# Two half blocks of y share their PSUM banks, and the image of both comes behind the products of both

## The chip, the cores and the metric

The kernel runs on one core of one Trainium2 chip. Its time is the device time of one execution in microseconds (us); the time before is the median of three runs. A profile is one further execution, taken by the hardware profiler, with start and duration of every instruction. The engines are TensorE (PE, with its weight loads shown apart as PEld), VectorE (DVE), ScalarE (ACT), GpSimd (POOL) and SyncE (SP, which only issues transfers here).

## The reference

The input x has 256 channels ("tokens") of 256 by 256 points, stored as (1, 256, 256, 128). Layer 0 is a gated attention with a residual sum; its result x1 goes to DRAM. Layer 1 is a Fourier neural operator on 256 tokens of 256 by 128 points. Cut to what matters here:

```
def spectral_conv(x, wr, wi, bias, out_hw):
    xf = rfft2(x); keep the low modes; mix them by w = wr + 1j * wi
    return irfft2(of) + bias
def fno_layer(x, ...):
    skip = einsum('bihw,oi->bohw', x, sw) + sb
    xf = spectral_conv(...); y = instance_norm(xf) + skip     # then gelu in the first of two
```

An attention over tokens comes first. In the kernel its skip part and the residual are folded into one matrix over tokens, mpT, and its spectral part into a small set of modes. Their sum is **y**, the quantity that the change is about: y = (mpT applied to x1) + (image of the modes), scaled per channel, together with the mean and variance of y for the norm that follows.

## The kernel before, in words

Everything is float32. Tokens stand on the 128 partitions, in two halves a = 0 and 1. A half of y has 32 half blocks u of 8 rows by 128 points (1024 columns, name HB), two of which are a block b of 16 rows (NB = 2048 columns).

`y_blocks` (line 1308) is a generator that makes one half block per step:

- **load**: two transfers on SP bring the half block of x1 for both token halves (tile xt, three buffers); for every even u four transfers bring the block's modes (tile gs, three buffers). They are asked for two half blocks ahead.
- **products** (line 1332): for each of four row classes j, two matmuls with 128 by 128 weights over 256 columns, summed in bank j. A float32 matmul shows as two records, so a half block has 16.
- **image** (line 1336, its matmul at line 1200): eight matmuls with 32 rows of weights, of which the four of different j run in different quarters of the array and write to four banks. Again 16 records.
- **eviction** (line 1342): DVE multiplies each bank's 256 columns by a row vector and writes to the kept array `blocks` (half 0) or to a tile yt (half 1, two buffers).
- **statistics** (line 1344): two bn_stats on DVE.
- **store** (line 1346, half 1 only): POOL issues a transfer of yt to the DRAM array yd.

The order of the work on each engine is the order in the program (`manual_schedule`). Half 0 runs alone, in a pool of eight banks, so two half blocks are in flight. Half 1 has one set of four banks ("r"), since the other four ("q") hold the modes' work. `weave(main, side)` (line 1231) mixes its half blocks into another generator: `main` yields the time that it expects PE to be free, `side` the time of its step, and steps of `side` are placed while time is due. The first 24 half blocks are woven into `first_modes(0)`: a chain of statistics, the mixing of modes (`mix_modes`, line 1349: 16 products named x0m, every third on POOL and the others on DVE, each summed by a matmul with the identity at line 1381, tile x0acc), the squares (x0sq) and norm (x0ens), and four chunks of synthesis (`synth_modes`, tile g10gp, line 576) with a small reduction at lines 1471 to 1489 behind the second chunk. What is left of the 24 runs alone. Then `first_images(0)` follows (line 1491: tile ups, ACT's gelu, a sum w of x1 and y with loads xw that use the buffers of yt). The last eight half blocks are woven into the start of `second_modes(0)` (line 1585: f1ps, z0m, z0acc).

Each step waits only by tile: a matmul that starts in a bank waits until that bank's last reader is done, an eviction into yt until the store of that buffer has landed.

Of the kernel before, what the change touches and what calls it, by code (L numbers as in the profile page):

```python
# [10 lines left out]
FP = mybir.dt.float32  # L11
AF = mybir.ActivationFunctionType
ALU = mybir.AluOpType
# [5 lines left out]
P = 128  # L19
# [3 lines left out]
def bc(ap, axis, n):  # L23

    a = ap.unsqueeze(axis)
    shape = list(a.shape)
    shape[axis] = n
    return a.to_broadcast(shape)
# [484 lines left out]
def layer1(tc, I, C, ident, x1d, upool, U, stats2, mv2, out):  # L513
# [6 lines left out]
    nc = tc.nc  # L520
    NT, H, W = 256, 256, 128
    L = lambda n: I["L1_conv_" + n]
    with ExitStack() as ctx:
# [10 lines left out]
        rwb = keep.tile([P, W], FP, name="rwb")  # L534
        bsy = keep.tile([P, W], FP, name="bsy")
# [112 lines left out]
        with tc.manual_schedule(engines=COMPUTE):  # L648
# [306 lines left out]
            ps = psa.tile([P, 512], FP, tag="a", name="gtps")  # L955
# [12 lines left out]
            mpT = late.tile([P, 2, NT], FP, name="mpT")  # L968

            for t in range(2):  # L970
                for b in range(2):
                    ps = psa.tile([P, 512], FP, tag="a", name=f"fvps_{t}_{b}")
# [19 lines left out]
        xp = yctx.enter_context(tc.tile_pool(name="xp", bufs=2))  # L992

        def load_x1(a, u):

            t = xp.tile([P, 2, NB // 2], FP, tag="xt", name=f"xt_{a}_{u}", bufs=3)
            for sc in range(2):
                nc.sync.dma_start(t[:, sc], x1v[:, sc, u * NB // 2 : (u + 1) * NB // 2])
            return t
# [109 lines left out]
        with tc.manual_schedule(engines=COMPUTE):  # L1109
# [33 lines left out]
            ps = psa.tile([P, 512], FP, tag="a", name="mbps")  # L1143
# [20 lines left out]
            for c in range(4):  # L1164
                ps = psa.tile([P, 512], FP, tag="a", name=f"fyps_{c}")
# [15 lines left out]
        ydv = yd.rearrange("(a p) x -> p a x", p=P)  # L1181
        outv = out.rearrange("(a p) h w -> p a (h w)", p=P)
        HB = NB // 2
        big = ctx.enter_context(tc.tile_pool(name="big", bufs=1, side="right"))
        blocks = big.tile([P, 16, NB], FP, name="blocks")
        hb = [blocks[:, b, :] for b in range(16)]

        def by_turn(t):

            return t.rearrange("p (n j w) -> p j n w", j=4, w=W)  # L1190

        def rows_of(ps):
            return ps.rearrange("p (n w) -> p n w", w=W)

        def image(ps, gs, bs, rows=range(4)):

            for k, n in enumerate(rows):
                for j in range(4):
                    q = slice(32 * j, 32 * j + 32)
                    nc.tensor.matmul(  # L1200
                        ps[j][:, k * W : (k + 1) * W], gs[q, n, :], bs[q, :],
                        start=False, stop=(k == len(rows) - 1),
                    )
# [16 lines left out]
        def load_modes(gs, Gd, b, tt=None):  # L1220
            for j in range(4):
                q = slice(32 * j, 32 * j + 32)
                if tt is None:
                    nc.sync.dma_start(
                        gs[q].rearrange("f n t -> f (n t)"),
                        Gd[:, j, 4 * b : 4 * b + 4, :].rearrange("f n t -> f (n t)"),
                    )
                else:
                    nc.sync.dma_start(gs[q], Gd[:, j, 4 * b : 4 * b + 4, tt])
# [19 lines left out]
        ystat = sp.tile([P, 2, 64, 6], FP, name="ystat")  # L1249
        with tc.tile_pool(name="psb", bufs=4, space=PSUM) as psa:  # L1250

            ps = psa.tile([P, 512], FP, tag="a", name="chps")
# [4 lines left out]
            ps = psa.tile([P, 512], FP, tag="a", name="blkps")  # L1257
# [50 lines left out]
        def y_blocks(a, psum, lo, hi, kept=16):  # L1308

            tt = slice(a * P, (a + 1) * P)  # L1310
            gs = {}

            def load(u):
                if (a, u) not in xts:
                    xts[a, u] = load_x1(a, u)
                if u % 2 == 0:
                    gs[u // 2] = xp.tile([P, 4, P], FP, tag="gs", name=f"gs_{a}_{u}", bufs=3)
                    load_modes(gs[u // 2], Gd0, u // 2, tt)

            load(lo)  # L1320
            load(lo + 1)
            yield 0.0
            for u in range(lo, hi):
                b, s = u // 2, u % 2
                if u + 2 < hi:
                    load(u + 2)
                xt = xts.pop((a, u))
                ps = [psum.pool.tile([P, 512], FP, tag=psum.tag, name=f"yps_{a}_{u}_{j}") for j in range(4)]
                ps = [z[:, 0:256] for z in ps]
                for j in range(4):  # L1330
                    for sc in range(2):
                        nc.tensor.matmul(  # L1332
                            rows_of(ps[j]), mpT[:, sc, tt], by_turn(xt[:, sc])[:, j],
                            start=(sc == 0), stop=False,
                        )
                image(ps, gs[b], bsy, range(2 * s, 2 * s + 2))
                if a == 0:
                    yt = blocks[:, b, s * HB : (s + 1) * HB]
                else:
                    yt = xp.tile([P, HB], FP, tag="yt", name=f"yt_{u}")  # L1340
                for j in range(4):
                    nc.vector.tensor_tensor(by_turn(yt)[:, j], rows_of(ps[j]), bc(rwb, 1, 2), ALU.mult)  # L1342
                for g in range(2):
                    nc.vector.bn_stats(ystat[:, a, 2 * u + g, :], yt[:, g * 512 : (g + 1) * 512])
                if a:
                    nc.gpsimd.dma_start(ydv[:, a, u * HB : (u + 1) * HB], yt)  # L1346
                yield 4.2

        def mix_modes(mk, acc, F, l, tag, cs):

# [445 lines left out]
        with tc.manual_schedule(engines=COMPUTE | {ENG.SP}):  # L1796
            with tc.tile_pool(name="psy", bufs=8, space=PSUM) as psy:
                run(y_blocks(0, Banks(psy, "y"), 0, 32))
# [6 lines left out]
            with yctx:  # L1805
                U1 = 24
                with tc.tile_pool(name="mp0", bufs=1) as wp:
                    y1 = y_blocks(1, br, 0, U1)
                    weave((2.4 * t for t in first_modes(0, wp, tiles(wp), bq, [(wp, "gt", 1)])), y1)
                    run(y1)  # L1810
                with tc.tile_pool(name="hp0", bufs=2) as wp:
                    run(first_images(0, wp, xp, bq, br))
                with tc.tile_pool(name="mp1", bufs=1) as wp:
                    y1 = y_blocks(1, br, U1, 32)
                    next(y1)
                    m0 = second_modes(
                        0, wp, tiles(wp), bq, [(xp, "xt", 3)], [(wp, "gt", 1)] * 3 + [(xp, "xt", 3)]
                    )
                    weave((2.4 * next(m0) for _ in range(3)), y1)
                    run(y1)  # L1820
                    m1 = first_modes(
                        1, wp, Tiles(F=(xp, "yt", 2), f=(xp, "yt", 2), m=(xp, "gs", 3)), br, [(xp, "xt", 3)]
                    )
                    next(m1)
                    for k, _ in enumerate(iter(lambda: next(m0), None)):
                        if k % 4 == 3:
                            next(m1)
                    for _ in m0:
                        next(m1, None)
                    o0 = output_0(bq)  # L1830
                    next(o0)
                    y2 = wp.tile([P, NB], FP, tag="gt", name="y2_0", bufs=1)
                    nc.sync.dma_start(y2, ydv[:, 1, 0:NB])
                    run(m1)
                    g2 = wp.tile([P, 4, P], FP, tag="m", name="gs2_1_0", bufs=2)
                    next(o0)
                    load_modes(g2, halves[1].Gd1, 0)
                    next(o0)
# [14 lines left out]
            with tc.tile_pool(name="op1", bufs=2, side="right") as op:  # L1853
                o1 = Output1(op)
                with tc.tile_pool(name="mp3", bufs=1) as wp, tc.tile_pool(
                    name="mpq3", bufs=8, space=PSUM
# [14 lines left out]
                with tc.tile_pool(name="opk1", bufs=8, space=PSUM) as psk, tc.tile_pool(  # L1871
                    name="op2", bufs=1
# [165 lines left out]
```

## Time and profile before

| what | value |
|---|---|
| median of three runs | 2890.68 us (2889.41 to 2895.76) |
| the profiled execution: its time | 2890.7 us |
| its span, first to last instruction | 2888.9 us |
| PE / DVE / ACT / POOL busy in the span | 2651 / 2008 / 1491 / 1680 us |
| half 0 of y | 1900.2 to about 2040 us |
| half 1, first 24 half blocks, woven and alone | 2039.6 to 2200.1 us |
| half 1, last eight half blocks | 2335.7 to 2390.6 us |
| line 1332, products of y | 1024 records, 247.7 us busy |

Times in the profile are us from the span's start, unless they are marked ns. A row of the timeline gives start, length, engine, line, operation, tiles, shape, and in square brackets how long the engine was idle before it and what ended that. A merged row of matmuls ends with the last one's drain, so its length exceeds the distance to the next row's start; distances between starts are used below. The granted clock is the share of TensorE's full clock. The chain that ended last spreads over very many short pieces (its largest entry is 5% of the span, PE), so the stretches have to be read one by one.

### The profile page before, as it was taken

Reading aid. Unit: us, or ns where it says so; the run is one execution under the profiler, and the core shown is the slowest. Engines: PE = TensorE matmul, PEld = TensorE weight load, DVE = VectorE, ACT = ScalarE, POOL = GpSimd, SP = SyncE. Lnnn points to the kernel's source line nnn. Section 1 sums busy time; section 2 is a strip of 40 time slices with the busy share of each in tenths; the row PEclk is TensorE's granted clock in tenths of the full one; section 3 lists DMA queues with packets and bytes.
Section 4 is the critical chain, followed back from the end, with each engine's and each line's share of the span. In section 5 each row is a group of like instructions: output and inputs, shape, how many; then the busy total and the mean of one; then the engine's idle time right before and its main releaser. Section 6 shows DMA issues by size and latency. Waiting matters only on the chain. (4 is left out here: it accounts for less than half of the span.)

```text
span 2888.9 us, 71477 instructions
## 1 busy us (share of the span) xinstructions
PE 2651.2 (92%) x29116; PEld 1941.7 (67%) x29116; DVE 2008.1 (70%) x3263; ACT 1491.0 (52%) x2849; POOL 1679.9 (58%) x1308
## 2 busy tenths in 40 slices
PE   6799999999999999999999899999889988799654
PEld 6677777777777777777777656778665555455532
DVE  7788888888888888888888744756645545365555
ACT  0477777777777777777777622200004611365132
POOL 0399999999999999999999800200114833111211
PEclk9999999999999999999999989999989989799865
DMA  9422222222222222222222101188879984798599
GB/s 369 164 67 67 67 67 67 67 67 67 67 68 69 68 67 69 68 66 71 67 67 67 41 19 53 34 278 271 277 236 319 310 296 137 251 360 305 187 359 337
DMA packets 246705, 430.12 MB, mean 149 GB/s; under 512 B 26278, under 2 KB 174201, under 8 KB 239976
## 3 DMA queue, kind: packets, MB, share of 16 engines
q1 hardware_dynamic: 206568, 335.34, 34.8%
q0 software_dynamic: 22912, 81.80, 7.4%
q10 hardware_dynamic: 16896, 8.39, 1.0%
q8 instruction: 231, 3.78, 0.5%
q14 instruction: 98, 0.80, 0.1%
HBM read 290.17 MB, written 135.27 MB: 147 GB/s over the span
## 5 line engine op out<-in xcount | busy, mean ns | idle before, releaser
L299 POOL TENSOR_TENSOR e<-e,b1T 128x1024 f32<-128x1024 f32 x256 | 606.0, 2367 | 165.3 <-PE u L348 90.4
L303 POOL TENSOR_TENSOR es<-e 128x512 f32<-128x512 f32 x512 | 639.4, 1270 | 20.1
L281 ACT ACTIVATE sc<-sc,b2T 128x512 f32<-128x512 f32 x512 | 339.0, 662 | 364.7 <-PE sc L272 356.4
L323 DVE RECIPROCAL av<-av 128x256 f32<-128x256 f32 x256 | 452.3, 1767 | 27.2 <-DVE og L322 1.4
L281 ACT ACTIVATE e<-sc,b2T 128x512 f32<-128x512 f32 x512 | 348.7, 681 | 0.0
L294 DVE TENSOR_TENSOR e<-sc,b1T 128x1024 f32<-128x1024 f32 x256 | 311.1, 1215 | 0.0
L272 PE MATMUL sc<-qkT 32*128 32x256 f32 x4096 | 293.5, 400 | 1.3 <-DVE e L294 1.3
L311 PE MATMUL av<-e,v 128*32 128x256 f32 x4096 | 274.7, 385 | 0.5 <-POOL e L299 0.5
L1332 PE MATMUL yps<-xt,mpT 128*128 128x256 f32 x1024 | 247.7, 396 | 17.8 <-DVE yt L1342 9.3
L272 PEld LDWEIGHTS sc<-qkT 32*128 32x128 f32 x4096 | 185.2, 184 | 112.3 <-issue 97.8
L322 DVE SCALAR_TENSOR_TENSOR og<-gate,av 128x256 f32<-128x256 f32 x256 | 107.7, 421 | 190.6 <-PE av L316 190.6
L1332 PEld LDWEIGHTS yps<-xt,mpT 128*128 128x128 f32 x1024 | 195.9, 196 | 56.8 <-DVE yt L1342 14.7
L1346 POOL DMA_DIRECT2D yd<-yt x32 | 17.8, 555 | 346.1 <-DVE yt L1342 346.1
L327 POOL TENSOR_TENSOR x<-xt,bo 128x256 f32<-128x256 f32 x256 | 187.5, 733 | 0.0
L246 PE MATMUL qk<-xnT,wT_wq 128*128 128x256 f32 x512 | 179.5, 432 | 1.7 <-ACT xnT L238 1.7
L252 PEld LDWEIGHTS gv<-wT_wv,kvT 128*128 128x128 f32 x1024 | 155.0, 192 | 13.4
L316 PE MATMUL av<-es,ones 128*32 128x256 f32 x2048 | 157.5, 379 | 2.6 <-POOL es L303 2.5
L333 PE MATMUL wo<-wT_wo,og 128*128 128x128 f32 x1024 | 156.8, 276 | 2.7 <-DVE og L324 2.7
L311 PEld LDWEIGHTS av<-e,v 128*32 128x32 f32 x4096 | 106.9, 109 | 76.1 <-POOL e L299 1.0
L348 PE MATMUL u<-adft,x 128*128 128x129 f32 x1024 | 156.4, 275 | 0.0
L252 PE MATMUL gv<-wT_wv,kvT 128*128 128x128 f32 x1024 | 156.0, 275 | 0.0
L1699 ACT ACTIVATE blocks<-h2ps,col 128x512 f32<-128x512 f32 x128 | 89.0, 776 | 129.5 <-PE h2ps L1200 129.5
(546 smaller groups left out, 5294.4 us busy)
## 6 DMA issues: line engine op xcount, KB each, us to landing
xt<-x1d SPq DMA_DIRECT2D x128, 512.0 KB
xb<-in_x_dram SPq DMA_DIRECT2D x32, 1024.0 KB
xt<-in_x_dram SPq DMA_DIRECT2D x128, 256.0 KB
kt<-in_L_conv_kv_x_dram SPq DMA_DIRECT2D x128, 256.0 KB
x1d<-x SPq DMA_DIRECT2D x256, 128.0 KB
y<-yd SPq DMA_DIRECT2D x62, 512.0 KB
gs<-Gd SPq DMA_DIRECT2D x384, 64.0 KB
yd<-yt POOLq DMA_DIRECT2D x32, 512.0 KB, 6.0
```

The costliest lines, as they stand in the source:

```text
L246: nc.tensor.matmul(ps[:, 0:256], wT["wq"], xnT, start=True, stop=True)
L252: nc.tensor.matmul(ps[:, 256 + c * P : 256 + (c + 1) * P], kvT[:, c * P : (c + 1) * P], wT["wv"], start=True, stop=True,)
L272: nc.tensor.matmul(sc[h // 2][:, h % 2, c * 256 : (c + 1) * 256], qkT[p, 256 + c * P : 256 + (c + 1) * P], qkT[p, 0:256], start=True, stop ...
L281: nc.scalar.activation(r["e"][1][:, :, c, :] if hp else z, z, AF.Exp, bias=b2T[:, c, s : s + 1])
L294: nc.vector.tensor_tensor(r["e"][0].rearrange("p h c q -> p (h c q)"), r.pop("sc").rearrange("p h x -> p (h x)"), b1T[:, 0:2].rearrange("p ...
L299: nc.gpsimd.tensor_tensor(e1, e1, b1T[:, 2:4].rearrange("p h c q -> p (h c q)"), ALU.mult)
L303: nc.gpsimd.tensor_tensor(r["es"][hp], e[:, :, 0, :], e[:, :, 1, :], ALU.add)
L311: nc.tensor.matmul(ps[hd, 0:256], r["v"][:, c, hd], r["e"][h // 2][:, h % 2, c, :], start=(c == 0), stop=(c == 1),)
L316: nc.tensor.matmul(ps[32 * h : 32 * h + 32, 256:512], self.ones, r["es"][h // 2][:, h % 2, :], start=True, stop=True,)
L323: nc.vector.reciprocal(rd, rd)
L327: nc.gpsimd.tensor_tensor(r["x1"], r["x"], bc(self.bo, 1, 2), ALU.add)
L1332: nc.tensor.matmul(rows_of(ps[j]), mpT[:, sc, tt], by_turn(xt[:, sc])[:, j], start=(sc == 0), stop=False,)
```

## The change

The banks are taken once per block, whole (512 columns). The first half block's step now issues only its products, into columns 0 to 255; the second's issues its products into columns 256 to 511, and then the image of all four rows (16 matmuls, 32 records). Only the first matmul of a bank has the start flag. Eviction, statistics and store follow for the whole block: half 0 has four evictions of 512 columns and four statistics per block; half 1 keeps tiles yt of a half block, so it has eight evictions of 256 columns (both tiles' for each bank in turn), four statistics and two stores. The expected times of the steps become 3.6 and 4.6 in place of 4.2 each, so the woven half blocks fall at other places.

```diff
-                ps = [psum.pool.tile([P, 512], FP, tag=psum.tag, name=f"yps_{a}_{u}_{j}") for j in range(4)]
-                ps = [z[:, 0:256] for z in ps]
+                if s == 0:
+                    ps = [psum.tile(f"yps_{a}_{b}_{j}") for j in range(4)]
                 for j in range(4):
                     for sc in range(2):
                         nc.tensor.matmul(
-                            rows_of(ps[j]), mpT[:, sc, tt], by_turn(xt[:, sc])[:, j],
-                            start=(sc == 0), stop=False,
+                            rows_of(ps[j])[:, 2 * s : 2 * s + 2], mpT[:, sc, tt], by_turn(xt[:, sc])[:, j],
+                            start=(s == 0 and sc == 0), stop=False,
                         )
-                image(ps, gs[b], bsy, range(2 * s, 2 * s + 2))
+                if s == 0:
+                    yield 3.6
+                    continue
+                image(ps, gs.pop(b), bsy)
                 if a == 0:
-                    yt = blocks[:, b, s * HB : (s + 1) * HB]
+                    yts = [hb[b]]
                 else:
-                    yt = xp.tile([P, HB], FP, tag="yt", name=f"yt_{u}")
+                    yts = [xp.tile([P, HB], FP, tag="yt", name=f"yt_{2 * b + t}") for t in range(2)]
+                n = 4 // len(yts)
                 for j in range(4):
-                    nc.vector.tensor_tensor(by_turn(yt)[:, j], rows_of(ps[j]), bc(rwb, 1, 2), ALU.mult)
-                for g in range(2):
-                    nc.vector.bn_stats(ystat[:, a, 2 * u + g, :], yt[:, g * 512 : (g + 1) * 512])
-                if a:
-                    nc.gpsimd.dma_start(ydv[:, a, u * HB : (u + 1) * HB], yt)
-                yield 4.2
+                    for t, yt in enumerate(yts):
+                        nc.vector.tensor_tensor(
+                            by_turn(yt)[:, j], rows_of(ps[j])[:, t * n : (t + 1) * n], bc(rwb, 1, n), ALU.mult
+                        )
+                for t, yt in enumerate(yts):
+                    for g in range(n):
+                        nc.vector.bn_stats(ystat[:, a, 4 * b + t * n + g, :], yt[:, g * 512 : (g + 1) * 512])
+                    if a:
+                        k = 2 * b + t
+                        nc.gpsimd.dma_start(ydv[:, a, k * HB : (k + 1) * HB], yt)
+                yield 4.6
```

## The prediction

> **What bounds the kernel now.** I read the page first: TensorE (PE) is busy for 2651 of 2889 us, and of the rows that the change touches the costliest is the product matmul.
>
> ```profile
> L1332 PE MATMUL yps<-xt,mpT 128*128 128x256 f32 x1024 | 247.7, 396 | 17.8 <-DVE yt L1342 9.3
> L1346 POOL DMA_DIRECT2D yd<-yt x32 | 17.8, 555 | 346.1 <-DVE yt L1342 346.1
> ```
>
> Then the busy time by stretches: half 0 of y alone (1900 to 2040), half 1 woven with the first mode mixing (to 2166), half 1 alone (to 2200), and its last eight half blocks (2343 to 2396).
>
> ```profile
> 1900.00:2040.00 140.00, 138.31 (x1026) 112.20 (x1027) 86.33 (x194) 0.00 (x0) 0.00 (x0) 1.00 0.85 278
> 2066.00:2121.00 55.00, 44.38 (x351) 29.50 (x351) 28.90 (x54) 1.99 (x4) 9.33 (x12) 0.96 0.60 213
> 2166.00:2200.00 34.00, 31.02 (x264) 24.77 (x249) 18.71 (x40) 3.26 (x4) 5.28 (x9) 1.00 0.91 317
> ```
>
> After the length come the busy times of PE, weight loads, DVE, ACT and POOL; the last three numbers are granted clock, DMA share and GB/s. Half 0 is PE alone. In the mixing PE idles for 10.6 us; in half 1 alone DMA is near its limit too. The timeline of PE in half 0:
>
> ```profile
> 1951.86 3.72 PE L1332 MATMUL yps<-xt,mpT 128*128 128x256 f32 x16
> 1955.51 0.73 PE L1200 MATMUL yps<-bsy,gs 32*128 32x128 f32 x16
> 1956.16 3.72 PE L1332 MATMUL yps<-xt,mpT 128*128 128x256 f32 x16
> ```
>
> and of the same image helper where 32 records stand together, in the next stage:
>
> ```profile
> 2208.43 1.17 PE L1200 MATMUL ups<-k_bsyn,gs 32*128 32x128 f32 x32
> 2209.53 0.33 PE L1553 MATMUL htps<-ident,blocks 128*128 128x128 f32 x1
> ```
>
> From start to next start 16 product records take 3.65 us, 16 image records 0.65, 32 image records 1.10. So 16 more image records cost 0.45, and 0.20 of each visit is fixed. The product side has a fixed part as well: in cut views the last five product records before an image take 1.17 us (1950.03 to 1951.20) and the last three 0.74 (from 1950.46), so one in the run costs 0.215 and 16 would be 3.45; the other 0.20 hangs on the neighbours. Each visit to the image thus costs 0.40 us beside its work.
>
> The woven stretch, all engines, at one of its five equal stalls:
>
> ```profile
> 2078.30 1.42 DVE L1342 TENSOR_TENSOR yt<-yps,rwb 128x256 f32<-128x256 f32 x4 [3.40 <-PE yps L1200]
> 2080.01 0.60 POOL L1346 DMA_DIRECT2D yd<-yt  x1 [7.02 <-DVE yt L1342]
> 2080.63 1.06 POOL L1368 TENSOR_TENSOR x0m<-F,mixwn 128x512 f32<-128x512 f32 x1
> 2081.74 1.12 PE L1381 MATMUL x0acc<-x0m,ident 128*128 128x512 f32 x2 [1.55 <-POOL x0m L1368]
> ```
>
> A product of the mixing waits on POOL behind the store of yt, which waits for DVE's last eviction. And what a longer stall does, one chunk of the same synthesis twice:
>
> ```profile
> 2117.07 3.72 PE L576 MATMUL g10gp<-x0Z,k_esyn 32*64 32x128 f32 x128 [2.94 <-ACT x0sq L1397]
> 2138.81 2.09 PE L576 MATMUL g10gp<-x0Z,k_esyn 32*64 32x128 f32 x128
> ```
>
> After 2.94 us idle PE runs at half speed for a while. Stalls of 1.5 us never did this here; 2.19 us at 2202 did.
>
> **What the Trainium skill says.** "TensorEngine Tiling (Array Packing)", section Tiling Modes: changing the tiling mode drains TensorE. The 0.40 us per visit agrees. "TensorE: Matmul & The Clock Gate", Part 1: the clock halves after an idle window of about 3.4 us, judged in free-running windows. The trace agrees in kind, though 2.19 us sufficed. "PSUM — Partial Sum Buffer", The four PSUM rules: a first matmul clears the flags of its whole bank, so later ones without the flag overwrite clear columns. One start per bank therefore suffices; no run here shows it yet.
>
> **The change, part by part.** "u" is a half block, "b" a block of two. PE's matmuls and their operands stay; half the visits to the image go. For half 0 evictions become four of 512 columns: rows of 256 (416 ns) and 1024 (1215 ns) put one at 0.68 us, and four in a row at 2.5 (four of 256: 1.42). The eight of half 1 take 2.8 (spacing 0.335), four statistics 2.5 (0.61 each). An image of 32 lets DVE start 1.18 us after its start.
>
> (A) Half 0. Sixteen visits fewer at 0.405: -6.5. The cover it needs is eviction (5.0 of 8.2 us per block, eight banks) and loads (278 GB/s becomes 291; each x tile has 8.2 us from slot to use, against about 3.5 of transfer). Half 1's first product waits for the last eviction of half 0: 2.5 instead of 1.42, +1.1. Sum -5.4.
>
> (B) The first five half blocks of half 1, with a single set of four banks. Before, PE stalls 0.50, 1.44, 0.89 and 0.50 behind evictions, and from 2039.57 to the sixth's start takes 25.7 us. After: two products 7.1, image 1.1, stall 0.9 (bank 0 needs two evictions), two products 7.1, image 1.1, broadcast 0.57, product 3.65 with 0.3 of stall: 21.8. DVE's aggregate and rsqrt chain starts 2.3 later after half 0's image, but ends as the first block's eviction begins (11.3 against 12.0 us after that image); its second part ends at 19.9, before PE's broadcast at 21.0. Sum -3.9.
>
> (C) The mixing. The order becomes: half 5 and image, M0 M1 M2, half 6, M3 M4, half 7 and image, M5 to M8, half 8, M9 M10, half 9 and image, M11 to M13, half 10, M14 M15, half 11 and image, synthesis. POOL has two stores ahead of M2's operand, each 0.55, and the later eviction: M2 stalls 3.1. DVE has 5.3 us of evictions and statistics ahead of M7's and M13's operands: they stall 1.18 + 5.2 + 0.75 - 3.05 = 4.1 each. Together 11.3. Before: 1.48, four of 1.55 and 2.94 before the synthesis, 10.6. Fewer mode changes give -0.4: net +0.3. The clock: before, the 2.94 cost 1.63 in the synthesis and 1.1 in the next product. After, three stalls are long enough. A fixed window gives for 4.1 us of idle 1.1 to 2.4, on average 1.6; three at nine in ten 4.5. Bounds: 0 and 8. Sum +0.3 + 4.5 - 2.75 = +2.1.
>
> (D) From the synthesis to 2200. Six images of 1.10 for twelve of 0.65, and neighbours: -2.3. Stalls: three of 0.93 for eight of 0.57, but the reduction at line 1474 waits for DVE behind a block's eviction, 5.1 for 2.6: +0.8. The stores: each pair is issued 2.7 and 3.3 us after the first eviction starts, and the next block's evictions, 9.1 later, need both buffers. A single store lands in 6.5 us here. I take +1.2 for two joints. Sum -0.3.
>
> (E) The hand-over at 2200. The first load of xw needs half 22's store landed; it came at 2200.0, as PE finished y. Now that store is issued at the last image + 3.9 and lands 6 us after PE has finished. The modes of image 1 are queued behind that load on SP, and PE wants them at +8.4: they would land near +10. Sum +1.7 (0 to 3).
>
> (F) The last four blocks. PE still waits for x half 26 until 2357.2; then three pairs win about 1.1 each, 3.35 in all. DVE's tail to the first z0m grows from 5.74 to 8.75 us after the last image's start, and the last pair of buffers is about 2 late, with DMA at 1.0:
>
> ```profile
> 2389.84 0.73 PE L1200 MATMUL yps<-bsy,gs 32*128 32x128 f32 x16
> 2395.58 2.07 PE L1381 MATMUL z0acc<-z0m,ident 128*128 128x256 f32 x4 [5.01 <-DVE z0m L1368]
> ```
>
> The last image's start moves from 2389.84 to 2386.5; sum -3.35 + 3.0 + 2 - 0.5 (x26 a little earlier) = +1.2.
>
> Total: -5.4 - 3.9 + 2.1 - 0.3 + 1.7 + 1.2 = -4.6. The profiled execution took 2890.7 (span 2888.9 and 1.8 around it), the median 2890.68: the forecast is 2886.1, and span 2884.3. Every later stage is moved as it is.
>
> **Rivals.** *Little is paid back*: no added clock loss in C (its sum -2.4 instead of +2.1) and landings as quick as the best (2.9 to 5 us, D and F 3 less): -4.6 - 4.5 - 3 = -12, or 2879. For: the windows' phase can be kind, and DVE has slack in most stretches. Against: 2.19 us of idle already halved the clock once.
>
> *The loads hide half 0's gain*: if 278 GB/s is what the queue gives with three x tiles, A's -6.5 vanishes: 2892.6. For: DMA share 0.85. Against: 335 to 349 GB/s elsewhere, and SP waits for PE there, not for landings. It equals the case that the drain isn't what costs the 0.40; against that stands the row of 32.
>
> *Slower, by the two yt buffers*: both are filled and stored together, so a block's eviction waits for the pair. It decides when the second store takes over 9 us, 2.1 per joint more than assumed at five joints (blocks 8 to 11, 13 to 15): +10.5, or 2896.6. For: landings up to 10.4 us near 2345, DMA share 1.0. Against: a late store also delays PE, and so the next loads.
>
> **How the numbers follow.** Forecast 0.45, own range 2882 to 2890; little paid back 0.28; loads 0.10; slower 0.17. A repeat measurement tells about 0.2%, 5.8 us: the forecast case lies beyond it with 0.20 of its 0.45. Faster 0.20 + 0.28 = 0.48, same 0.25 + 0.10 = 0.35, slower 0.17. The range 2878 to 2896 leaves out the ends of the first and third rival.
>
> **What would show it.** Right: half 0 at 8.2 us per block, PE busy throughout; image rows x32 at 1.17; stalls of about 3 and twice 4 us at the mixing's matmuls, with slow products after them; the reduction at 5 us; first xw load 6 us after y. Wrong: products in pairs at over 7.1 us with a full clock; DVE evictions waiting for DMA by over 2 us per block; no half-speed products before 2120.

## The result and the profile after

| | before | after |
|---|---|---|
| median | 2891.12 us (2889.41 to 2895.76) | 2909.09 us (2905.39 to 2912.90) |
| ratio of the times | | 1.0055, interval 1.004 to 1.007 |
| the profiled execution: time, span | 2890.7, 2888.9 us | 2912.9, 2911.1 us |
| PE / DVE / ACT / POOL busy | 2651 / 2008 / 1491 / 1680 us | 2645 / 1994 / 1491 / 1682 us |

The changed kernel is about half a per cent slower; the forecast was 2886.1, with 2896 as its upper end. In a later comparison of the same two kernels it was again slower, by a ratio of 1.0033 (1.0024 to 1.0042). By the medians the change costs 18 us in the first comparison and 9 us in the later one; the first profile of the changed kernel was taken in the slowest of its four runs.

TensorE (PE) is busy for less time than before. From the costliest groups of the changed kernel (after the bar: busy us and mean ns, then the idle time before them):

```profile
L1332 PE MATMUL yps<-xt,mpT 128*128 128x256 f32 x1024 | 242.8, 396 | 19.4 <-DMA xt<-x1d 8.6
```

The same products take 5 us less. The busy times by stretches, the same three windows as before:

```profile
1900.00:2040.00 140.00, 137.14 (x1045) 116.42 (x1045) 82.15 (x134) 0.77 (x1) 0.00 (x0) 0.99 0.90 285
2066.00:2121.00 55.00, 43.15 (x220) 29.56 (x220) 21.90 (x46) 1.78 (x3) 8.59 (x11) 0.88 0.53 179
2166.00:2200.00 34.00, 30.56 (x331) 25.54 (x330) 16.64 (x38) 3.26 (x4) 6.29 (x10) 0.95 0.90 306
```

Half 0 stays a stage of PE alone. In the mixing (second line) the granted clock fell from 0.96 to 0.88, and the first synthesis, whose 128 records lay in this window before, now begins behind its end. The waits of PE from 2040 to 2206 say where it idled (us in total, times, the longest):

```profile
PE x0acc L1390 <- DVE x0m L1377: 7.7, 2, 3.9
PE x0rsp L1483 <- DVE bl L1480: 5.0, 1, 5.0
PE x0acc L1390 <- POOL x0m L1377: 4.2, 1, 4.2
PE yps L1332 <- issue: 3.6, 2, 2.1
PE g10gp L576 <- issue: 2.6, 1, 2.6
PE yps L1332 <- PE yps L1200: 2.6, 3, 0.9
PE g10gp L576 <- DVE col L1425: 2.5, 1, 2.5
```

In the same stretch before, PE waited often and briefly:

```profile
PE x0acc L1381 <- POOL x0m L1368: 7.7, 5, 1.6
PE yps L1332 <- DVE yt L1342: 7.3, 12, 1.4
PE g10gp L576 <- ACT x0sq L1397: 2.9, 1, 2.9
PE x0rsp L1474 <- DVE bl L1471: 2.6, 1, 2.6
```

The totals are not far apart: over all rows of the two views, also the short ones left out here, PE waited 29.0 us against 24.6. What differs is the lengths: in this stretch of y two waits exceed 2 us before, and seven after. (Another, of 2.19 us, follows y in both kernels.) The timeline of PE in the mixing shows what follows a long wait:

```profile
2070.11 2.08 PE L1390 MATMUL x0acc<-x0m,ident 128*128 128x512 f32 x2 [4.18 <-POOL x0m L1377]
2071.98 5.47 PE L1332 MATMUL yps<-xt,mpT 128*128 128x256 f32 x16
2077.29 1.88 PE L1390 MATMUL x0acc<-x0m,ident 128*128 128x512 f32 x4
...
2089.51 3.60 PE L1390 MATMUL x0acc<-x0m,ident 128*128 128x512 f32 x4 [3.87 <-DVE x0m L1377]
...
2108.61 1.12 PE L1390 MATMUL x0acc<-x0m,ident 128*128 128x512 f32 x2 [3.87 <-DVE x0m L1377]
2109.57 5.30 PE L1332 MATMUL yps<-xt,mpT 128*128 128x256 f32 x16
```

Sixteen product records take 3.62 us at full clock here, and 5.47 and 5.30 behind the waits. Four records of x0acc take 1.88, and 3.60 behind the second wait.

In the table below PE's time from the start of y is cut at landmarks, for the first profile of each kernel, and for one taken later (runs `e8_changed_again` and `e12_before_again`). The letters are the prediction's steps.

| step, from one first matmul to the next | forecast | before, again | after, again |
|---|---|---|---|
| A: y to the first product of half 1 | -5.4 | 139.4, 139.4 | 133.9, 133.9 |
| B: to the image of half block 5 | -3.9 | 29.4, 29.4 | 28.3, 25.4 |
| C: to the product of half block 12 | +2.1 | 57.8, 56.6 | 63.3, 58.7 |
| D: to the end of y's last image | -0.3 | 73.3, 72.2 | 78.8, 76.0 |
| E: to the first htps | +1.7 | 9.5, 9.5 | 15.1, 15.1 |
| image stage, to half block 24 | 0 | 126.1, 130.6 | 129.3, 130.8 |
| F: to the first z0acc | +1.2 | 59.9, 55.7 | 59.6, 61.3 |
| the rest | 0 | 493.3, 497.1 | 502.2, 496.6 |

Image stage and F make 186.1 and 186.3 in the two profiles of before, although each alone moved by over 4 us, so they are read together.

### The profile page after: what moved, and what is told of

It is laid out like the page before. It is cut to its first block, busy times and chain, and to the rows that moved or that the text cites. A ratio compares the mean times of both kernels' runs of the same rounds, so it can differ in the third digit from the quotient of the medians.

```text
span 2911.1 us, 71407 instructions
## 1 busy us (share of the span) xinstructions
PE 2645.3 (91%) x29116; PEld 1942.9 (67%) x29116; DVE 1994.4 (69%) x3199; ACT 1491.4 (51%) x2849; POOL 1681.8 (58%) x1308
## 5 line engine op out<-in xcount | busy, mean ns | idle before, releaser
L1332 PEld LDWEIGHTS yps<-xt,mpT 128*128 128x128 f32 x1024 | 199.8, 198 | 58.5 <-issue 15.5
```

The lines of the kernel that those rows point to most:

```text
L1332: nc.tensor.matmul(rows_of(ps[j])[:, 2 * s : 2 * s + 2], mpT[:, sc, tt], by_turn(xt[:, sc])[:, j], start=(s == 0 and sc == 0), stop=False,)
```

## The experiments

The stages of every profile (us; "to hand-over" runs from the first synthesis matmul to the end of y's first 24 half blocks, "to z0acc" takes step E, the image stage and F together). The start of y itself varies between 1894 and 1904 us, which is layer 0's and not counted.

| kernel | half 0 | to mixing | mixing | to hand-over | to z0acc | rest |
|---|---|---|---|---|---|---|
| before, again | 137.6, 137.6 | 31.8, 31.8 | 47.5, 47.5 | 83.0, 80.7 | 195.5, 195.8 | 493.3, 497.1 |
| after, again | 131.1, 131.1 | 32.2, 29.3 | 57.1, 55.0 | 83.8, 78.6 | 204.0, 207.2 | 502.2, 496.7 |
| e1: half 0 only | 131.1 | 32.8 | 47.5 | 79.9 | 196.2 | 492.8 |
| e2: half 1 only | 137.6 | 28.6 | 55.4 | 79.5 | 209.8 | 496.8 |
| e3: statistics later | 131.1 | 29.7 | 49.4 | 77.0 | 207.8 | 495.7 |
| e4: first xw elsewhere | 131.1 | 31.0 | 53.0 | 77.5 | 203.7 | 492.9 |
| e5: e3 and e4 | 131.1 | 30.4 | 47.4 | 79.2 | 204.6 | 494.1 |
| e6: e5, ACT stores | 131.1 | 29.3 | 43.1 | 75.5 | 200.8 | 493.0 |
| e7: e1 and e4 | 131.1 | 34.5 | 47.5 | 80.1 | 192.8 | 492.6 |
| e9: before, xw, ACT stores | 137.6 | 31.8 | 41.7 | 80.5 | 192.9 | 499.7 |
| e10: e7, ACT stores | 131.1 | 34.5 | 41.7 | 79.2 | 192.8 | 495.9 |
| e11: e6 again | 131.1 | 30.2 | 43.1 | 76.7 | 198.5 | 494.2 |

### Which half loses

One half in the new form, the other in the old (e1: `a == 0`, e2: `a == 1`):

```diff
+                if a == 0:
+                    ... whole block, as changed
+                else:
+                    ... half block, as before
```

> Half 0 of y in whole banks as in the changed kernel, half 1 as before the change. Theory 1 (the loss sits in half 1, where a block's evictions and statistics stand ahead of the mode chain on DVE): half 0 wins about 6.5 us in PE, 1.1 go back at the hand-over to half 1; 5 us faster than before, about 2886, and the stages behind are moved as they are. Theory 2 (the faster reading of x1 and the whole-bank form disturb the transfers, and later stages lose too): half 0 is 6.5 us shorter all the same, but the stages after 2690 us are longer, and the time is that of before or above, 2891 to 2898.

> Half 1 of y in whole banks as in the changed kernel, half 0 as before the change. Theory 1: about 6 us above the changed kernel, 2914 to 2917, with the same stalls of about 4 us in the mixing, about 5 at the reduction, and the same late start of the images. Theory 2: half 0's share of the loss is missing, so it is at or below the changed kernel's 2909.

e1 took 2887.76 us (12 runs; ratio to before 0.9993, 0.9979 to 1.0007), e2 2905.51 (8 runs; 1.0044, 1.0028 to 1.006). The loss belongs to half 1, and the stages show it. In e1 half 0 takes 131.1 us and the mixing 47.5, as before; in e2 half 0 takes 137.6 and the mixing 55.4. From y's start to z0acc e1 is 7.8 us shorter than the first profile of before and e2 15.5 longer. Theory 2, that half 0's new form makes later stages longer, falls: in e1 they take what they take before (196.2 and 492.8). Whole times tell less. The ratio of e1 does not exclude no change. The time of e2 is below the 2914 to 2917 of theory 1, and it is not measurably slower than the second measurement of the changed kernel, which has half 0's gain. The waits of PE in e2 (2034 to 2200) are those of the changed kernel:

```profile
PE x0acc L1412 <- DVE x0m L1399: 7.7, 2, 3.9
PE x0rsp L1505 <- DVE bl L1502: 5.0, 1, 5.0
PE x0acc L1412 <- POOL x0m L1399: 3.0, 1, 3.0
```

### DVE's burst

DVE has eight evictions (2.7 us) and four statistics (2.5) in one piece, and the mixing's next products behind them. Here the statistics of half 1 go into the next step, behind the next half block's products:

```diff
+                    if a and u > lo:
+                        for z, part in late:
+                            nc.vector.bn_stats(z, part)
                     yield 3.6
...
+                if a == 0 or u + 1 == hi:
+                    for z, part in late:
+                        nc.vector.bn_stats(z, part)
```

> The changed kernel, but in half 1 the four statistics of a block are issued one step later, behind the next half block's products, so only 2.7 us of evictions stand between the image and the mode chain on DVE instead of 5.2. Theory 1: the stalls at the seventh and thirteenth mixing matmul drop from 3.9 to about 1.4, those at the second chunk of the synthesis (2.5) and at the reduction (5.0) by 2.5 each, and the halved clock behind them goes with some of them: 10 us shorter from 2065 to 2205, time about 2899. If the loss between 2065 and 2205 comes from the transfers instead (stores in pairs, loads of x1): stalls may move, but the time stays at 2905 to 2912.

e3 took 2892.04 us (12 runs; 1.0003, 0.9989 to 1.0016). That is 0.0030 below the changed kernel's later ratio, or some 9 us; the expectation had 2899. The waits of PE in e3, 2034 to 2200:

```profile
PE x0acc L1398 <- POOL x0m L1385: 3.6, 2, 3.2
PE x0acc L1398 <- DVE x0m L1385: 3.0, 2, 1.5
...
PE x0rsp L1491 <- DVE bl L1488: 2.5, 1, 2.5
```

The two waits of 3.87 for DVE's operands are 1.5, the one of 4.96 is 2.5, and that for line 1425 is gone. The mixing takes 49.4 for 57.1 and 55.0. What is moved is the same work, so its place in DVE's queue, not its amount, made these waits. The one for POOL stays, as it does not stand behind the statistics. The stretch to z0acc stays long (207.8): moving the statistics did not mend that part.

### The hand-over

The first two pieces of xw were loaded into the buffers of yt, behind the last block's stores. Here they get a buffer of the tag xt, whose loads are over:

```diff
+                if b == 0:
+                    first_x = yp.tile([P, NB], FP, tag="xt", name="xw_0", bufs=3)
...
+                    if b == 0:
+                        ys[b, s] = first_x[:, s * HB : (s + 1) * HB]
```

> The changed kernel, but the first two pieces of xw go into a tile of xt, which is free early, so their load no longer waits for the last pair of stores of yt, and the modes of image 1 behind it on the SP queue come in time. If the hand-over at 2205 costs what the trace shows (5.5 us between the end of y and the first transpose), the time falls by 4 to 6 us, to about 2904, and the wait of 4.8 us at the second image goes. If that wait is only put in the place of another (DMA full): no change, 2907 to 2911.

> The changed kernel with both repairs: statistics of half 1 one step later, and the first pieces of xw in a tile of xt. If the two losses are separate, the repairs add: the first gave 0.5% back, the second 0.3%, so the time falls to 0.3% below before, about 2884, with stalls of 1.5 at the mixing's seventh and thirteenth matmul and 9 us from the end of y to the first transpose. If the image stage, full with transfers, takes back what comes earlier: about before, 2890 to 2893.

e4 took 2899.31 us (17 runs; 1.0024, 1.0015 to 1.0034), e5, with both edits, 2885.75 (6 runs; 0.9968, 0.9953 to 0.9982). In the changed kernel the hand-over reads like this, from the timeline of all engines:

```profile
2203.76 1.17 PE L1200 MATMUL yps<-bsy,gs 32*128 32x128 f32 x32
2207.65 1.06 POOL L1355 DMA_DIRECT2D yd<-yt  x2 [9.75 <-DVE yt L1347]
2210.74 1.02 SPq L1520 DMA_DIRECT2D xw<-x1d  x2
2211.80 2.70 SPq L1224 DMA_DIRECT2D gs<-Gd  x4
2217.23 2.78 PE L1200 MATMUL ups<-k_bsyn,gs 32*128 32x128 f32 x32 [4.77 <-DMA gs<-Gd]
2219.93 3.19 PE L1562 MATMUL htps<-ident,blocks 128*128 128x128 f32 x16
```

SP gets past the load of xw at 2210.7, where before it did at 2200.0; only then does it ask for the modes gs, and PE waits 4.77 us for them. In e4 the same load and the same modes are asked for at 2180.1 and 2180.9, 7 us before PE ends y (at 2187.0), and the first htps comes 8.6 us after y in place of 15.1. The gain to z0acc is smaller (203.7 against 204.0 and 207.2; e5 against e3 204.6 and 207.8): part of what the hand-over wins, the image stage and the last blocks take back. By the ratios to before, e4 gains 0.0009 on the 1.0033 of the changed kernel's later comparison (some 3 us for the 4 to 6 expected, and within the intervals) and e5 0.0035 on e3 (10 us). The profile of e5 shows only 2.3 of these 10 us between the start of y and z0acc; where the others are is not shown.

### The stores' queue

Half 1's stores asked for by ACT, which is nearly idle there (1.8 us busy of the mixing's 55), in place of POOL:

```diff
-                        nc.gpsimd.dma_start(ydv[:, a, k * HB : (k + 1) * HB], yt)
+                        nc.scalar.dma_start(ydv[:, a, k * HB : (k + 1) * HB], yt)
```

> As the one before, but the stores of yt are issued on ACT's queue instead of POOL's, so the POOL product of the mixing no longer stands behind two stores. The stall at the third mixing matmul falls from 3.0 to about 1 us or less, and the halved clock behind it goes: 3 us less than the one before, about 2881. If ACT's own chain (square roots, copies of the synthesis) is now late behind the stores, the stalls come back at the synthesis, and the time is that of the one before or above.

> Half 0 in whole banks, half 1 as before the change, the first pieces of xw in a tile of xt. Before the change the load of xw waited for the store of half block 22 only until y was done, so the repair has little to win here: 0 to 1 us beside half 0 alone, 2886 to 2889. If it wins 3 us or more, the hand-over was late before the change too.

e6 took 2877.13 us (5 runs; 0.9946, 0.9921 to 0.997), e7, with half 0 alone in the new form, the xw edit and POOL's stores, 2884.28 (5 runs; 0.9966, 0.995 to 0.9982). e7 was expected to win 0 to 1 us on e1. It wins 3.5 by the medians, though the intervals of the two ratios overlap, so the old half 1 may profit from the xw edit too. Its profile shows no gain at the hand-over (9.3 us, 9.4 in e1) and 3 us in the image stage (127.1 for 130.2), which moved by 4.5 us between the two profiles of before. In e6 the wait for POOL in the mixing is gone; the first long wait of the changed kernel, 4.18, is now

```profile
2065.23 1.12 PE L1398 MATMUL x0acc<-x0m,ident 128*128 128x512 f32 x2 [0.38 <-DVE yt L1350]
```

The edits of e5 and e6 could help the old half 1 as well, so e6's gain is not yet the block's. Three more runs tell it apart.

> y entirely in the old form of half blocks, with the two repairs that do not need the new form: the first two pieces of xw in a free buffer of x, and the stores of half 1 asked for by ScalarE in place of GpSimd. Half 0 must stay at 137.6 us. Theory 1 (a store ahead of a product of the mixing on GpSimd is what made five stalls of 1.5 us before): the stalls at line 1381 fall to under 0.6 us each, the mixing takes 41 to 43 us for 47.5, and the kernel takes 2881 to 2886 us. Theory 2 (the stalls come from VectorE's eviction, the store only passes them on): the stalls stay over 1.2 us and the time stays within 2888 to 2893.

> As the run before it, with half 0 in the new form of blocks and half 1 in the old. Theory 1: another 6.5 us less in half 0 (131.1 us), so 2875 to 2880 us. Theory 2: half 0 takes 131.1 us, but the image stage gives part of it back and the time is within 3 us of the run before it.

> The same kernel as e6_later_xw_act_store, next to the two runs before it: both halves in blocks, statistics of half 1 issued behind the next half block's products, the xw pieces and the stores as there. If the block form of half 1 pays once its waits are gone, it is 3 us or more below the run with half 0 alone in the new form; if whole blocks in half 1 only trade mode changes for longer bursts, it is within 3 us of it.

e9 (y in the old form, with xw and ACT stores) took 2884.39 us (12 runs; 0.9976, 0.9962 to 0.9991), e10 (half 0 in blocks) 2877.86 (5 runs; 0.9945, 0.9926 to 0.9965), e11 (both halves in blocks) 2878.93 (8 runs; 0.9964, 0.9949 to 0.9978). The waits of PE in e9:

```profile
PE x0acc L1381 <- POOL x0m L1368: 1.9, 5, 0.4
```

The five waits of the kernel before, 7.7 us in all, are 1.9: they came from the store on POOL ahead of the operand, with its own wait for the eviction, as the first theory had it. Half 0 in blocks is worth 6.5 us (e10 against e9, in its stage as in the medians; the intervals of the two ratios just overlap). Half 1 gives some of this back as it starts, so that 5.2 us are left at z0acc. And half 1 in blocks is worth nothing that these runs show: e11 is within 3 us of e10, and the intervals overlap. By stages it wins 5.4 us up to the hand-over (30.2 + 43.1 + 76.7 against 34.5 + 41.7 + 79.2) and loses 5.7 from there to z0acc. PE's waits for the modes in the image stage (2195 to 2350) go the same way (first e10, then e11):

```profile
PE ups L1200 <- DMA gs<-Gd: 1.3, 2, 1.0
```

```profile
PE ups L1200 <- DMA gs<-Gd: 4.7, 5, 2.2
```

In the changed kernel this row had 10.4 us. Another 2.4 us of the 5.7 stand at the end of F: ahead of the first z0acc PE waits 7.40 us for DVE in e11 and 5.01 in e10, as the last block's burst still stands in front of the second mixing's products. The queue of ACT has its price too: at the hand-over ACT's first gelu stands behind the last store, and the first wait of e10 for it is 4.4 us where e7, with POOL's stores, has 2.2; the first htps comes 12.1 us after y, in e7 9.3. The image stage (122.9 for 127.1) gives that back.

So e10 is the version to keep: half 0 in blocks, half 1 as before, and the two repairs. It beats both kernels; e6 and e11, which are one kernel, are its equal within what these runs tell.

### What is chance

> The changed kernel once more, beside the others. All theories: 0.4 to 0.7% above before. What it tells apart: the stretch behind 2690 us, 8 us longer in its first profile than before the change, is the change's if it is long again, and is chance if it is within 3 us of before's.

> The kernel before, unchanged, profiled a second time, to tell how far one stretch moves by itself. If the differences between the two profiles of the changed kernel (mixing 57.1 and 55.0, synthesis to hand-over 83.8 and 78.6, the stretch behind the second image's modes 502.2 and 496.7 us) are chance of the clock, a second profile of before moves by 1 to 5 us in its stretches too: mixing 46 to 50, synthesis to hand-over 79 to 84, hand-over with image stage 134 to 140, the last stretch 492 to 500, with half 0 fixed at 137.6. If before repeats to within 1 us everywhere, the differences belong to the change.

e8, the changed kernel again, took 2904.35 us (20 runs; 1.0033, a little under the 0.4 to 0.7% expected); e12, the kernel before again, 2892.59 (18 runs; 0.9999, 0.9985 to 1.0013). The second profile of the changed kernel has the same waits for DVE (3.87, 3.87, 4.96, 2.46) as the first, yet it is 2.9 us shorter in B, 4.6 in C and 2.7 in D. Three things differ. The first is the clock: the first pair of half 1 stood behind the same wait and ran at full clock in e8 (first row), but not in the first profile (the rows after it):

```profile
2037.28 7.17 PE L1332 MATMUL yps<-xt,mpT 128*128 128x256 f32 x32 [2.56 <-DVE blocks L1347]
```

```profile
2034.60 8.86 PE L1332 MATMUL yps<-xt,mpT 128*128 128x256 f32 x32 [2.55 <-DVE blocks L1347]
...
2121.08 2.04 PE L576 MATMUL g10gp<-x0Z,k_esyn 32*64 32x128 f32 x123
2125.75 0.44 PE L576 MATMUL g10gp<-x0Z,k_esyn 32*64 32x128 f32 x5 [2.62 <-issue]
2126.11 5.41 PE L1332 MATMUL yps<-xt,mpT 128*128 128x256 f32 x16
```

The record of the granted clock says why. In each profile it changes only at the edges of a fixed grid of 3.41 us, and the grid lies elsewhere in each execution. These rows give PE's busy time and the granted clock (the value behind POOL's count) in neighbouring stretches of the grid, first in the first profile, then in e8:

```profile
2031.36:2034.77 3.41, 0.86 (x28) 0.67 (x22) 2.67 (x5) 0.00 (x0) 0.00 (x0) 1.00 0.99 338
2034.77:2038.18 3.41, 3.41 (x9) 2.66 (x10) 3.38 (x5) 0.00 (x0) 0.00 (x0) 0.50 0.48 141
```

```profile
2032.39:2035.80 3.41, 2.33 (x38) 1.73 (x36) 1.06 (x2) 0.00 (x0) 0.00 (x0) 1.00 1.01 315
2035.80:2039.21 3.41, 1.93 (x9) 1.73 (x10) 3.38 (x7) 0.00 (x0) 0.00 (x0) 1.00 0.94 319
2039.21:2042.63 3.42, 3.42 (x18) 3.01 (x17) 2.56 (x3) 0.72 (x1) 0.00 (x0) 1.00 0.31 56
```

In the first profile the whole wait fell into one stretch, and the next one ran at half clock. In e8 an edge cut the wait into 1.08 and 1.48 us, and the clock stayed full.

The second is the gap of 2.62 inside the first synthesis (the row at 2125.75 above), which is absent in e8. The third is the landing of stores: in the first profile DVE waited 1.12 us at 2055 and 1.09 at 2065 for a store of half 1, which is why the third pair and the first mixing stall are longer there. In e8 it did not wait at either place.

The expectation of e12 that before would move by itself holds for the stretches with loads and for the last one: the image stage 126.1 and 130.6, the rest 493.3 and 497.1. Half 0, the way to the mixing and the mixing repeat to 0.1. So the rest's +8.9 in the first profile of the changed kernel is not shown to be the change's, and the second profile does not repeat it; over all profiles the kernels with half 1 in blocks lie at 492.9 to 502.2 in it, those with half 1 as before at 492.6 to 499.7. What stays are the 10.3 us from the start of y to z0acc (the means of 508.2 and 501.1, against 495.4 and 493.3). The later medians differ by 9.

## Why the prediction was wrong

Up to z0acc the sum was -4.6 us, and the means of two profiles of each kernel give +10.3. Of the 14.9 us between them 4.9 are step D's, 3.9 step E's, 3.1 the image stage and F together, 1.7 step C's and 1.3 step B's; A came within 0.1. So three terms failed: D left out a wait, E made one too short, and "every later stage is moved as it is" put the image stage at nothing. The clock loss, which was priced in C alone, comes on top in B, D and E.

**A** was right: -5.4 foreseen, -5.5 in both profiles. Half 0 runs at 8.2 us per block, as these three lines of the changed kernel's timeline of PE show:

```profile
1908.86 7.17 PE L1332 MATMUL yps<-xt,mpT 128*128 128x256 f32 x32
1915.97 1.17 PE L1200 MATMUL yps<-bsy,gs 32*128 32x128 f32 x32
1917.07 7.17 PE L1332 MATMUL yps<-xt,mpT 128*128 128x256 f32 x32
```

The rows' starts are 8.21 apart, 7.11 of products and 1.10 of image. The 0.40 us per visit held in every kernel with half 0 in blocks (131.1 in all ten profiles), and the rival of the loads falls with it: the queue gave 285 GB/s.

**B** was right in e8 (-4.0 for -3.9). In the first profile it was -1.1: the wait of 2.55 halved the clock for one window (8.86 for 7.17, 1.7 us), and the third pair came 1.2 late behind DVE's wait of 1.12 for a store. The step allowed for no clock loss behind the wait that it had itself put at 2.5.

**C** named its stalls well: about 3 and twice 4.1, measured 4.18 and 3.19 for the first in the two profiles, and 3.87 twice in both. Its sum, +2.1, lies between +0.9 (e8) and +5.5. In e8 waits are 10.9 (before 11.1, with the 0.50 ahead of half block 12) and clock losses 5.1 for a forecast of 4.5 (three times nine tenths of 1.6, the forecast's own factors, would be 4.3). What is left over, put down to the fewer mode changes, gave 1.6 rather than 0.4, and the first synthesis took 0.5 longer at full clock. In the first profile the unforeseen 2.62 of the synthesis comes on top, with a first stall that is 1.0 longer and clock losses of 6.2. That the sum lies between the two is in part luck, as the errors of its terms offset each other.

**D** failed (-0.3 for +5.4 and +2.7). The reduction's stall was right (5.1 foreseen, 4.96). Overlooked was a wait at the second synthesis chunk, in the timeline of the changed kernel:

```profile
2145.29 1.98 PE L576 MATMUL g10gp<-x0Z,k_esyn 32*64 32x128 f32 x116 [2.46 <-DVE col L1425]
...
2195.00 8.83 PE L1332 MATMUL yps<-xt,mpT 128*128 128x256 f32 x32 [2.14 <-issue]
```

Its later records start in a bank that x0ens held, and x0ens is read by DVE's small chain at line 1425, now behind a whole block's burst. The trace of before has that dependency with no idle time in it, which is why a reading of the waits alone did not show it. In e8 this wait also halved the clock, for another 1.35 us. With the statistics moved (e3) it is gone. The second line is the pair of stores: DVE waited 1.17 us for a store to land, and its stall of 2.14 in place of 0.87 is about the +1.2 that the step had. In the first profile it also cost 1.7 us of half clock, and so did the 2.62 us in the first synthesis, whose slow product stands at the start of D (5.41 us). In e8 the stall was 1.74 and the clock stayed full.

**E** failed by size (+1.7 with 0 to 3 for +5.6, in both). The first load of xw was foreseen 6 us after PE's end of y, and came 5.9 after it. Wrong was what follows: the modes were to land near +10, but were asked for at +6.9 and landed at +12.4, 5.4 us after the request; and half clock behind the 4.77 wait took another 2.8 us (2.78 for 1.17, 3.19 for 1.96).

**The later stages were not moved as they are.** The sum put the image stage at nothing, without a reason of its own. Image stage and F took 186.1 and 186.3 before, and 189.0 and 192.1 after, against a forecast of +1.2. PE's waits for gs in the image stage and hand-over, 1.4 us (6.2 in e12) before, are 10.4 and 9.0. That modes stand behind xw on SP had been said for image 1 only. The late start accounts for part: with the xw edit, e4 to e6 and e11 still take 198.5 to 204.6 us to z0acc, where half 1 as before takes 192.8. Of these 6 to 12 us 2.4 are the longer wait ahead of the first z0acc, which F had foreseen (3.0). What the rest is made of is not settled. The pairs of stores are a candidate that no run tried alone.

Of the rivals, *slower by the two yt buffers* had the right sign and the wrong place: DVE waited for stores 5.0 us in all in the first profile, at four places instead of five joints of 2.1, and the larger loss stands where SP waits for the stores. *Little is paid back* needed a kind clock; e8 had that in B and was still slower. The chance of slower, 0.17, was too low: B, D and E priced a wait without the half clock behind it, D also missed a reader queued behind the burst, E had the modes land 2.4 us too early, and each such omission has the same sign.

## What to carry to other kernels

Here larger pieces of work saved their fixed cost only where nothing else stood in the queues behind the pieces. Where two streams share an engine, the largest piece of one is the wait of the other; so halve the cost where a stage runs alone (half 0), and keep the pieces small where it is woven (half 1), or issue the part of the piece that nobody waits for later. Before a buffer's release is made later, list every queue in which an instruction waits for that buffer, and what stands behind it there, one step further than the first reader. And where a new wait is over about 2 us, add to its price the 1.7 us that half clock behind it may cost.

## What the runs showed of the hardware

- Whether a wait halves PE's clock depends on how much of it falls into one stretch of the grid of 3.41 us, not on its length alone. Between the start of y and 2210 us the fourteen profiles have 1209 stretches at full clock. In 40 of them PE stood for over 2.2 us, and half clock followed all 40. It followed 18 of the 20 with 1.8 to 2.2 us, and 5 of the 1149 with less. So the same 2.55 us cost 1.7 us in one execution and nothing in another, and 2.46 us cost nothing in one and 1.35 in the other. In e10 a wait of 2.94 us lay across an edge, with 1.5 us on each side, and cost nothing. The five waits of 1.5 in the kernel before cost nothing, while 1.50 and 0.44 us in one stretch of e3 were followed by half clock (a product row of 4.64 for 3.62). Many losses come to 1.7 us (1.69, 1.67, 1.68), which is half speed for one stretch. "TensorE: Matmul & The Clock Gate", Part 1, of the Trainium skill speaks of an idle window of about 3.4 us in free-running windows: the grid agrees, but here some 2 us of idle time inside one window were enough.
- In the first synthesis PE stopped after 123 of 128 small matmuls for 2.62 us in the first profile of the changed kernel, 2.33 in e3 and 2.5 in e5 and e11. In e8, the same program, record 124 came only 0.4 us after record 123. No semaphore released it ("issue"). The DMA records point to PE's own program: its 124th record starts 1.2 to 1.6 us after the end of a 16 KB packet of the queue that the page calls "instruction", in all seven profiles with both halves in blocks (the changed kernel's two, e3 to e6 and e11). In the first profile this packet began at 2123.3, when PE had already stopped; in e8 it had ended before PE came to the place. That PE waited for this packet is argued, not shown, and why it came late is open.
- A store costs POOL's queue 0.55 us and the wait for its data, and five products of the mixing behind one each had cost PE 5.8 us (7.7 less 1.9). On ACT, which had nothing else to do in the mixing, this is gone; it comes back where ACT has work, 2.8 us at the hand-over.
